# Forward column transform of a Fourier layer over three chunks of rows, each PSUM block with a member (index f) of its own, in place of two chunks with partial sums

## The chip, the cores and the metric

The kernel runs on one core of one Trainium2 chip. A core has five engines that run side by side and meet through semaphores: TensorE (PE in the profile; its weight loads have a row of their own, PEld), VectorE (DVE), ScalarE (ACT), GpSimd (POOL) and SyncE (SP, which here only issues DMAs). TensorE reads its operands from the on-chip memory SBUF and writes its results to the accumulation memory PSUM, from where VectorE or ScalarE has to copy ("evict") them.

The metric is the device time of one execution in microseconds (us). Before the change it is 3847.83 us, the median of three runs (3844.99 to 3849.62). The execution that the profile comes from took 3850.84 us, with a span of 3849.0 us from its first to its last instruction.

## The reference

The input is a batch of 8 images of 8 channels and 256x256 pixels. Two blocks are applied, each with a residual. The first is a grouped Fourier network (4 groups of 10 channels), the second a 3x3 maximum filter:

```python
x = x + fourier_net(group_norm(x))
x = x + dilate3x3(group_norm(x))

def fourier_net(x):                      # 4 groups, 2 channels each, plus two coordinate planes
    h = gconv1x1(concat(x, grid), fc0_w, fc0_b)               # 10 channels per group
    for i in range(4):
        xf = rfft2(h)                                         # only 24 x 12 low modes are used
        lo = einsum('bgixy,gioxy->bgoxy', xf[..., :12, :12], w1[i])
        hi = einsum('bgixy,gioxy->bgoxy', xf[..., -12:, :12], w2[i])
        h = irfft2(place(lo, hi)) + gconv1x1(h, w_w[i], w_b[i])
        if i < 3:
            h = gswish(h)
    h = gswish(gconv1x1(h, fc1_w, fc1_b))                     # 128 hidden channels per group
    return gconv1x1(h, fc2_w, fc2_b)
```

All of it is in float32. Because so few modes are kept, the Fourier transforms are done as products with small tables of cosines and sines.

## The kernel before, in words

**Stages.** Each image goes through four layers. A layer begins with its small spectral part: `spectrum_h` (row transform of what the layer before left in `zt`, L356 and L366), `mix` (the products with the mode weights, L394 and L397) and `rows_of` (inverse row transform into `zt`, L456 or L462, copied by L207). Then comes the loop of `layer` over NCH = 11 chunks of rows, which is where the change is. After the fourth layer the image's state is stored to DRAM, and its head (the 128 hidden channels, fc1 and fc2) is computed later, in 128 steps.

**Two images at once.** The head of image b is not run by itself. `layers` of image b+1 is a generator that yields at marked places, and the driver loop at the end of the kernel answers each `yield (1,)` with one step of the head that is waiting, and each `yield "tail"` with one piece of the dilation of the image before that. So the order on each engine is written out by hand through these yields; the engines take their instructions in exactly this order. The first image has no head beside it (the flag `alone[0]` is true), and after the last image's layers its own head is all that is left.

**A head step** is `first(n)`: four matmuls of 512 columns (L736) into four PSUM banks, evicted by ScalarE in two instructions (L737 one bank, L738 three banks). Every second step, those with odd n, is followed by `second`: eight matmuls (L751) into one bank, which VectorE adds up (L760).

**PSUM.** The eight banks are handed out as two tags with two buffers each: `one` (one bank) and `tri` (three banks). `ps_four` takes one of each. The two buffers of a tag are used in turn, so a user of `tri` waits until the user before the last one has been evicted. A chunk's `burst`, a `first`, a `transform` each take a `one` and a `tri`; `gather` and `second` take a `one` alone.

**The chunk loop.** For each chunk c, `burst(c)` computes the layer's output for that chunk: 16 small matmuls for the 1x1 convolution (L539 in layer 0, L542 in the others) and 8 for the inverse column transform (L545, which reads `zt`), all into one `ps_four`. ScalarE evicts them through the activation into `h` (L550: one instruction of 512 elements per partition, one of 1536). `turn(c)` transposes that chunk in blocks of 32x32 on VectorE (L493, two instructions) into slot c % 3 of `turned`.

The forward column transform then takes two chunks at a time. `transform(k)` runs 32 matmuls of 32 rows by 32 columns (L510). The 256 pixels of a row are split into 8 sections of 32 (index v). Section v goes to the block of 32 PSUM partitions v % 4, so each block gathers only two of the eight sections: four partial sums come out side by side. They are copied to SBUF (L513 on VectorE, L514 on ScalarE), into the third slot of `turned`. `gather(k)` adds the four partial sums with the table `stack` (four identities on top of each other): 4 matmuls over all 128 rows (L524), whose result VectorE copies into `zt` (L527, or L530 twice where the chunks' slots are out of order). With 11 chunks there are five pairs and one single chunk. The same product also brings channel groups and pieces f into the places that the next layer wants: `group_in_f` is true in layers 1 (and 3), false in layers 0 and 2.

Each fp32 matmul is two PE instructions in the trace (a high and a low part), each with its own weight load; counts in the profile are twice those in the code.

Of the kernel before, what the change touches and what calls it, by code (L numbers as in the profile page):

```python
# [21 lines left out]
G = 4  # L22
# [22 lines left out]
def fno_dilate_kernel(ctx: ExitStack, tc: tile.TileContext, a: dict, out: bass.AP):  # L45
# [440 lines left out]
    def layer(b, l, out_, stored, side):  # L486
# [9 lines left out]
        def chunks_of(k):  # L496

            return sorted(range(2 * k, min(2 * k + 2, NCH)), key=lambda c: c % 3)

        def transform(k):  # L500


            cs = chunks_of(k)
            n, lo = len(cs), cs[0] % 3
            step = cs[-1] % 3 - lo if n == 2 else 1
            t = turned[:, lo : lo + step * (n - 1) + 1 : step].rearrange("p n (r v i) -> p n r v i", r=2 * NQ, v=8)
            one, tri, banks = ps_four(f"p_d_{b}_{l}_{k}")
            for v in range(8):
                for q in range(NQ):
                    mm(banks[q][part(v % 4), : 240 * n], fw8[part(q), v, :],  # L510
                       t[part(q), :, :, v, : NBLK * WID], start=v < 4, stop=v >= 4)
            e = turned[:, (2 * k + 1) % 3, : 960 * n].rearrange("p (q x) -> p q x", q=NQ)
            nc.vector.tensor_copy(e[:, 0], one[:, : 240 * n])  # L513
            nc.scalar.activation(e[:, 1:4], tri[:, :, : 240 * n], AF.Identity)  # L514

        def gather(k):

            cs = chunks_of(k)
            n = len(cs)
            e = turned[:, (2 * k + 1) % 3, : 960 * n].rearrange("p (q r f i) -> p q r f i", q=NQ, r=2 * n, f=NQ)  # L520
            p = ps_a(f"p_u_{b}_{l}_{k}")
            for g in range(NQ):
                m = e[:, :, :, g].rearrange("p q r i -> p r q i") if group_in_f else e[:, g]
                mm(p[part(g), : 240 * n], stack, m, start=True, stop=True)  # L524
            src = p[:, : 240 * n].rearrange("p (r g i) -> p r g i", r=2 * n, g=G)
            if cs == sorted(cs):
                nc.vector.tensor_copy(zt[:, 4 * k : 4 * k + 2 * n, :, : NBLK * WID], src)  # L527
            else:
                for i, c in enumerate(cs):
                    nc.vector.tensor_copy(zt[:, 2 * c : 2 * c + 2, :, : NBLK * WID], src[:, 2 * i : 2 * i + 2])  # L530
# [45 lines left out]
        for k in range((NCH + 1) // 2):  # L576
            c = 2 * k
            pair = c + 1 < NCH
# [465 lines left out]
```

## Time and profile before

| | |
|---|---|
| time, median of 3 runs | 3847.83 us (3844.99 to 3849.62) |
| the profiled execution | 3850.84 us, span 3849.0 us |
| PE busy | 3620.7 us (94%), 54200 matmul instructions and as many weight loads |
| DVE busy | 2423.8 us (63%) |
| ACT busy | 2832.3 us (74%) |
| POOL busy | 117.0 us (3%) |
| mean granted PE clock | 0.972 of full speed |
| chain that ended last | PE 76%, DVE 14%, issue 5%, ACT 4%, DMA 1% |
| L510, transform | 9216 instructions, 308.6 us busy |
| L524, gather | 1152 instructions, 136.7 us busy |
| L513 and L514, its evictions | 144 each; ACT 182.9 us |

"Busy" is the time in which at least one instruction of the kind is running; matmuls overlap, so a PE that is shown busy can still be slowed down by what it waits for. "Idle before" a group is the time that the engine stood still just before its instructions, with the engine that ended most of it. The chain that ended last is followed back from the last instruction, at each step to what released it.

By time, a layer's chunk loop takes 53.8 us in all layers 1 and 2 of the images from the second on (first eviction of a burst to the last), and the small spectral part between two loops takes about 63 us. For the first image, which has no head beside it, they take 35.3 us and 43 to 47 us. The last image's layers end at 3551.0 us; the rest is its head.

### The profile page before, as it was taken

Reading aid. Unit: us, or ns where it says so; the run is one execution under the profiler, and the core shown is the slowest. Engines: PE = TensorE matmul, PEld = TensorE weight load, DVE = VectorE, ACT = ScalarE, POOL = GpSimd, SP = SyncE. Lnnn points to the kernel's source line nnn. Section 1 sums busy time; section 2 is a strip of 40 time slices with the busy share of each in tenths; the row PEclk is TensorE's granted clock in tenths of the full one; section 3 lists DMA queues with packets and bytes.
Section 4 is the critical chain, followed back from the end, with each engine's and each line's share of the span. In section 5 each row is a group of like instructions: output and inputs, shape, how many; then the busy total and the mean of one; then the engine's idle time right before and its main releaser. Section 6 shows DMA issues by size and latency. Waiting matters only on the chain.

```text
span 3849.0 us, 119276 instructions
## 1 busy us (share of the span) xinstructions
PE 3620.7 (94%) x54200; PEld 1347.2 (35%) x54200; DVE 2423.8 (63%) x3893; ACT 2832.3 (74%) x2919; POOL 117.0 (3%) x202
## 2 busy tenths in 40 slices
PE   5668999999999999999999999999999999999997
PEld 2333333333333333333333333333333333333222
DVE  6775665556775666766666676665676566673633
ACT  2435777777777777787777777777777777778986
POOL 1000000000000000000000000000000000000100
PEclk7878999999999999999999999999999999999998
DMA  3005111432225222361123612144222532225321
GB/s 88 15 28 193 48 47 45 150 107 61 65 85 178 77 61 61 99 200 55 49 64 110 193 56 58 44 145 154 61 63 59 178 99 63 65 64 182 114 54 51
DMA packets 114089, 345.11 MB, mean 90 GB/s; under 512 B 15984, under 2 KB 18480, under 8 KB 98160
## 3 DMA queue, kind: packets, MB, share of 16 engines
q1 hardware_dynamic: 95392, 276.32, 23.4%
q0 software_dynamic: 18192, 61.17, 5.0%
q8 instruction: 426, 6.98, 0.7%
q14 instruction: 79, 0.65, 0.1%
HBM read 213.43 MB, written 123.74 MB: 88 GB/s over the span
## 4 chain that ended last, share of the span: by engine, by line
PE 76%; DVE 14%; issue 5%; ACT 4%; DMA 1%; POOL 0%; DVEq 0%; POOLq 0%; ACTq 0%
PE p_fc L736 20%; PE p_fc L751 19%; PE p_z L545 10%; PE p_d L510 8%; PE p_z L542 8%; PE p_u L524 3%; PE p_z L539 3%; DVE S L397 3%; DVE turned L394 3%; PE p_b L366 2%; DVE y L760 2%; PE p_g L462 2%; ACT act L738 2%; DVE turned L356 1%; ACT act L737 1%
## 5 line engine op out<-in xcount | busy, mean ns | idle before, releaser
L738 ACT ACTIVATE act<-p_fc 128x1536 f32<-128x1536 f32 x1024 | 1492.6, 1458 | 36.1 <-PE p_fc L736 35.0
L736 PE MATMUL p_fc<-hs,c_w 32*128 32x512 f32 x8192 | 1227.4, 633 | 49.9 <-ACT act L738 13.5
L751 PE MATMUL p_fc<-act,c_w 128*32 128x512 f32 x8192 | 996.1, 602 | 2.0 <-issue 2.0
L737 ACT ACTIVATE act<-p_fc 128x512 f32<-128x512 f32 x1024 | 615.4, 601 | 360.1 <-PE p_fc L736 347.0
L493 DVE STREAM_TRANSPOSE turned<-h 128x1024 f32<-128x1024 f32 x528 | 633.9, 1226 | 250.7 <-ACT h L550 249.9
L550 ACT ACTIVATE h<-p_z 128x512 f32<-128x512 f32 (+1 forms) x528 | 511.9, 1022 | 265.4 <-PE p_z L545 265.4
L736 PEld LDWEIGHTS p_fc<-hs,c_w 32*128 32x128 f32 x8192 | 388.1, 185 | 666.4 <-ACT act L737 230.2
L760 DVE TENSOR_TENSOR y<-p_fc,y 128x512 f32<-128x512 f32 x392 | 267.1, 681 | 551.2 <-PE p_fc L751 551.2
L751 PEld LDWEIGHTS p_fc<-act,c_w 128*32 128x32 f32 x8192 | 215.6, 109 | 713.3 <-issue 376.3
L545 PE MATMUL p_z<-c_binv,zt 32*128 32x256 f32 x5632 | 415.5, 410 | 0.4
L542 PE MATMUL p_z<-h,c_wt 32*32 32x512 f32 x8448 | 367.3, 604 | 6.1 <-ACT act L737 4.2
L545 PEld LDWEIGHTS p_z<-c_binv,zt 32*128 32x128 f32 x5632 | 261.6, 189 | 312.8 <-issue 296.6
L510 PE MATMUL p_d<-turned,c_fw 32*32 32x480 f32 (+1 forms) x9216 | 308.6, 540 | 4.3 <-PE p_z L545 2.9
L514 ACT ACTIVATE turned<-p_d 128x1440 f32<-128x1440 f32 x144 | 182.9, 1270 | 95.2 <-PE p_d L510 92.0
L552 ACT ACTIVATE h<-p_z,c_bias 128x512 f32<-128x512 f32 (+1 forms) x176 | 186.5, 1110 | 76.0 <-PE p_z L545 75.8
L207 DVE COPY zt<-p_g 128x264 f32<-128x264 f32 x304 | 154.7, 604 | 76.6 <-PE p_g L462 46.5
L397 DVE TENSOR_REDUCE S<-turned 128x80 f32<-128x800 f32 x192 | 188.8, 983 | 5.7
L394 DVE TENSOR_TENSOR turned<-t,B 128x800 f32<-128x800 f32 x192 | 188.4, 981 | 0.1
L510 PEld LDWEIGHTS p_d<-turned,c_fw 32*32 32x32 f32 x9216 | 128.2, 103 | 170.2 <-issue 65.1
L356 DVE STREAM_TRANSPOSE turned<-zt 128x960 f32<-128x960 f32 x96 | 177.0, 1870 | 2.9 <-DVE zt L527 0.5
L542 PEld LDWEIGHTS p_z<-h,c_wt 32*32 32x32 f32 x8448 | 92.4, 103 | 188.8 <-ACT act L737 66.6
L524 PE MATMUL p_u<-turned,c_stack 128*32 128x480 f32 (+1 forms) x1152 | 136.7, 543 | 7.2 <-DVE turned L513 6.2
(182 smaller groups left out, 1742.8 us busy)
## 6 DMA issues: line engine op xcount, KB each, us to landing
stored<-h SPq DMA_DIRECT2D x88, 1024.0 KB
hs<-stored SPq DMA_DIRECT2D x352, 256.0 KB
t<-in_spw SPq DMA_DIRECT2D x96, 400.0 KB
yin<-y_rows POOLq DMA_DIRECT2D x56, 512.0 KB, 5.2
h<-in_xp SPq DMA_DIRECT2D x352, 48.0 KB
turned<-in_xw SPq DMA_DIRECT2D x16, 1024.0 KB
y<-in_x SPq DMA_DIRECT2D x56, 256.0 KB
y_rows<-y POOLq DMA_DIRECT2D x56, 256.0 KB, 3.9
```

The source lines that it names most:

```text
L394: nc.vector.tensor_tensor(pr, sw[k], bt[:, k2, k].unsqueeze(2).to_broadcast([128, G, 2 * WID, WID]), ALU.mult)
L397: nc.vector.tensor_reduce(s[k2][:, k].rearrange("p s o g -> p (s o) g"), pr.rearrange("p g m i -> p m g i"), AX.X, ALU.add,)
L493: nc.vector.transpose(dst[:, 2 * i : 2 * i + 2], h[:, c, 2 * i : 2 * i + 2].rearrange("p f (s x) -> p f s x", s=2))
L510: mm(banks[q][part(v % 4), : 240 * n], fw8[part(q), v, :], t[part(q), :, :, v, : NBLK * WID], start=v < 4, stop=v >= 4)
L542: mm(o, wt[part(q), l, g, :], h[part(q), c, f, :], start=True, stop=False)
L545: mm(banks[q][:, HW * s : HW * (s + 1)], zt[part(q), 2 * c + s].rearrange("p f o -> p (f o)"), binv[part(q), :], start=False, stop=s == 1)
L550: nc.scalar.activation(dst, src, AF.Silu)
L736: mm(banks[g], w1[part(g), blk, :], hs[k][part(g), :], start=True, stop=True)
L737: nc.scalar.activation(act[:, 0, :], one, AF.Silu)
L738: nc.scalar.activation(act[:, 1:4, :], tri, AF.Silu)
L751: mm(acc[part(g), :], w2[:, g, 15 - rb - i : 47 - rb - i], act[:, g, :], start=i == 0, stop=i == 1)
L760: nc.vector.tensor_tensor(y, sums, y, ALU.add)
```

## The change

`transform` now takes three chunks at a time (three, three, three and two). A chunk holds four pieces of two pixel rows each (index f). The block of 32 PSUM partitions is now chosen by f, no longer by v % 4, and all eight sections v accumulate in it. So there are no partial sums and `gather` is gone. In place of 32 matmuls with 480 columns for two chunks there are 128 with 180 columns for three.

In layer 1 the result is then already where `zt` wants it, and `put` copies it there (VectorE one bank, ScalarE three). In layers 0 and 2 channel group and piece f have to change places: the result is first copied to SBUF (`swapped`, in slot 2 of `turned`), and the new `swap` sends it once more through TensorE, 16 matmuls of 32x32 with the identities of `stack`, into a further `ps_four`, which `put` then copies to `zt`.

The loop is rewritten to fit. With a head beside it, one chunk is handled per round with one head step each (from the second chunk on); `transform(k - 1)` stands after the step of the first chunk of the next three, ahead of that chunk's `turn`, and `swap(k - 1)` after the step of the second chunk. The number of head steps in a layer's loop and after it is the same, 12; the `"tail"` yields are 11 per layer, before 10. For the first image, `transform(k - 1)` stands after the second chunk's burst, and the first chunk's `turn` is put off until after it.

```diff
--- before.py
+++ after.py
@@ -495,39 +495,51 @@
 
         def chunks_of(k):
 
-            return sorted(range(2 * k, min(2 * k + 2, NCH)), key=lambda c: c % 3)
+            return range(3 * k, min(3 * k + 3, NCH))
+
+        def put(k, one, tri):
+
+            rs = slice(2 * chunks_of(k)[0], 2 * chunks_of(k)[-1] + 2)
+            dst = zt[:, rs, :, : NBLK * WID]
+            n = 60 * len(chunks_of(k))
+            nc.vector.tensor_copy(dst[:, :, 0], one[:, :n].rearrange("p (r i) -> p r i", i=NBLK * WID))
+            nc.scalar.activation(
+                dst[:, :, 1:4].rearrange("p r g i -> p g r i"),
+                tri[:, :, :n].rearrange("p g (r i) -> p g r i", i=NBLK * WID), AF.Identity)
+
+        def swapped(k):
+
+            return turned[:, 2, : 240 * len(chunks_of(k))].rearrange("p (q x) -> p q x", q=NQ)
 
         def transform(k):
 
 
-            cs = chunks_of(k)
-            n, lo = len(cs), cs[0] % 3
-            step = cs[-1] % 3 - lo if n == 2 else 1
-            t = turned[:, lo : lo + step * (n - 1) + 1 : step].rearrange("p n (r v i) -> p n r v i", r=2 * NQ, v=8)
+            n = len(chunks_of(k))
+            t = turned[:, :n].rearrange("p n (s f v i) -> p (n s) f v i", s=2, f=NQ, v=8)
             one, tri, banks = ps_four(f"p_d_{b}_{l}_{k}")
             for v in range(8):
                 for q in range(NQ):
-                    mm(banks[q][part(v % 4), : 240 * n], fw8[part(q), v, :],
-                       t[part(q), :, :, v, : NBLK * WID], start=v < 4, stop=v >= 4)
-            e = turned[:, (2 * k + 1) % 3, : 960 * n].rearrange("p (q x) -> p q x", q=NQ)
-            nc.vector.tensor_copy(e[:, 0], one[:, : 240 * n])
-            nc.scalar.activation(e[:, 1:4], tri[:, :, : 240 * n], AF.Identity)
-
-        def gather(k):
-
-            cs = chunks_of(k)
-            n = len(cs)
-            e = turned[:, (2 * k + 1) % 3, : 960 * n].rearrange("p (q r f i) -> p q r f i", q=NQ, r=2 * n, f=NQ)
-            p = ps_a(f"p_u_{b}_{l}_{k}")
-            for g in range(NQ):
-                m = e[:, :, :, g].rearrange("p q r i -> p r q i") if group_in_f else e[:, g]
-                mm(p[part(g), : 240 * n], stack, m, start=True, stop=True)
-            src = p[:, : 240 * n].rearrange("p (r g i) -> p r g i", r=2 * n, g=G)
-            if cs == sorted(cs):
-                nc.vector.tensor_copy(zt[:, 4 * k : 4 * k + 2 * n, :, : NBLK * WID], src)
+                    for f in range(NQ):
+                        mm(banks[q][part(f), : 60 * n], fw8[part(q), v, :],
+                           t[part(q), :, f, v, : NBLK * WID], start=v == 0, stop=v == 7)
+            if group_in_f:
+                put(k, one, tri)
             else:
-                for i, c in enumerate(cs):
-                    nc.vector.tensor_copy(zt[:, 2 * c : 2 * c + 2, :, : NBLK * WID], src[:, 2 * i : 2 * i + 2])
+                e = swapped(k)
+                nc.vector.tensor_copy(e[:, 0], one[:, : 60 * n])
+                nc.scalar.activation(e[:, 1:4], tri[:, :, : 60 * n], AF.Identity)
+
+        def swap(k):
+
+            if group_in_f:
+                return
+            e = swapped(k)
+            one, tri, banks = ps_four(f"p_u_{b}_{l}_{k}")
+            for j in range(NQ):
+                for g in range(NQ):
+                    mm(banks[g][part(j), : 60 * len(chunks_of(k))], stack[part(g), :], e[part(g), j],
+                       start=True, stop=True)
+            put(k, one, tri)
 
         def burst(c):
             one, tri, banks = ps_four(f"p_z_{b}_{l}_{c}")
@@ -573,44 +585,40 @@
                 if c > 3 and not alone[0]:
                     read_x(b + 1, c - 4)
             return
-        for k in range((NCH + 1) // 2):
-            c = 2 * k
-            pair = c + 1 < NCH
+        for c in range(NCH):
+            k, i = divmod(c, 3)
             burst(c)
-            if k > 1:
-                gather(k - 2)
             if alone[0]:
+                if k > 0 and i == 1:
+                    transform(k - 1)
+                    turn(c - 1)
+                if k > 0 and i == 2:
+                    swap(k - 1)
+                if k == 0 or i:
+                    turn(c)
+                if c == NCH - 1:
+                    swap(k - 1)
+                continue
+            if c == 0:
+                yield "tail"
                 turn(c)
-                if pair:
-                    burst(c + 1)
-                if k > 0:
-                    transform(k - 1)
-                if pair:
-                    turn(c + 1)
                 continue
-            if k == 1:
-                transform(0)
-            if k > 0:
+            if k > 0 and i == 0:
                 yield (1,)
+                transform(k - 1)
+                turn(c)
             else:
-                yield "tail"
-            turn(c)
-            if k > 1:
-                transform(k - 1)
-            if k > 0:
-                for _ in range(2 if pair else 1):
-                    yield "tail"
-            if pair:
-                burst(c + 1)
-                turn(c + 1, (0,))
-            yield (1,)
-            if pair:
-                turn(c + 1, (1,))
+                turn(c, (0,))
+                yield (1,)
+                turn(c, (1,))
+            yield "tail"
+            if k > 0 and i == 1:
+                swap(k - 1)
         out_["sw"] = [load_sw(l + 1, k) for k in range(3)]
-        gather(k - 1)
-        transform(k)
         yield (1,)
-        gather(k)
+        transform(3)
+        yield (1,)
+        swap(3)
 
     def start(b, out_):
         if b < n_img:
```

## The prediction

> **What bounds the kernel now.** First the page: shares, clock and chain.
>
> ```profile
> span 3849.0 us, 119276 instructions
> ...
> PE 3620.7 (94%) x54200; PEld 1347.2 (35%) x54200; DVE 2423.8 (63%) x3893; ACT 2832.3 (74%) x2919; POOL 117.0 (3%) x202
> ...
> PE 76%; DVE 14%; issue 5%; ACT 4%; DMA 1%; POOL 0%; DVEq 0%; POOLq 0%; ACTq 0%
> ```
>
> TensorE is the bound, but the change sits in the chunk loop, so I asked for the busy times of one such loop (image 4, layer 1) and of the stretch after it.
>
> ```profile
> 1873.70:1927.50 53.80, 53.60 (x929) 20.46 (x925) 40.08 (x49) 43.60 (x44) 3.13 (x5) 1.00 0.17 51
> 1927.50:1990.10 62.60, 60.56 (x734) 21.16 (x733) 39.28 (x63) 46.00 (x48) 0.54 (x1) 1.00 0.23 67
> ```
>
> After the stretch come its length and the busy us of PE, PEld, DVE, ACT and POOL, then the clock. In the loop PE has no gap, full clock; DVE and ACT have 10 us to spare. Next the timeline of two chunks in that loop (start, length; PE and ACT rows).
>
> ```profile
> 1892.66 1.14 PE L736 MATMUL p_fc<-hs,c_w 32*128 32x512 f32 x8
> ...
> 1893.73 2.19 PE L510 MATMUL p_d<-turned,c_fw 32*32 32x480 f32 x58
> ...
> 1894.32 1.45 ACT L738 ACTIVATE act<-p_fc 128x1536 f32<-128x1536 f32 x1
> ...
> 1895.37 0.59 PE L542 MATMUL p_z<-h,c_wt 32*32 32x512 f32 x1
> ...
> 1895.80 1.28 PE L542 MATMUL p_z<-h,c_wt 32*32 32x512 f32 x31
> ...
> 1897.98 1.04 PE L736 MATMUL p_fc<-hs,c_w 32*128 32x512 f32 x8
> ...
> 1898.17 1.94 ACT L550 ACTIVATE h<-p_z 128x512 f32<-128x512 f32 x2 [0.74 <-PE p_z L545]
> ...
> 1898.95 1.92 PE L751 MATMUL p_fc<-act,c_w 128*32 128x512 f32 x16
> ```
>
> Start to start, a burst costs PE 2.17 us (L542 1.10, L545 1.07), a first 1.07, a second 1.85 (1898.95 to 1900.80), a gather 0.95. ACT needs 1.94 us for a burst and 1.95 for a first. The two L542 lines matter most: the burst issued one matmul and then stood until 1895.80, just after ACT's L738 ended at 1895.77. That is the `tri` rule: a unit waits for the eviction of the unit before the last. Before the change this costs little, because each pair of chunks is gather, first, transform, burst, first, second, burst: between a unit and the next but one there is always about 2 us of other PE work.
>
> Last, how fast 32x32 matmuls stream (timeline rows of four whole groups).
>
> ```profile
> 2316.21 1.49 PE L462 MATMUL p_g<-c_rowg,fz 32*32 32x66 f32 x128
> ...
> 2188.45 0.88 PE L419 MATMUL p_f<-fs,c_fold 32*32 32x72 f32 x64
> ...
> 1933.49 1.44 PE L510 MATMUL p_d<-turned,c_fw 32*32 32x240 f32 x64
> ...
> 1927.47 2.29 PE L510 MATMUL p_d<-turned,c_fw 32*32 32x480 f32 x64
> ```
>
> Record by record, in the first and the last two of these 17 matmuls go out (34 weight loads), then PE pauses; the 18th goes out 0.33, 0.62 and 1.02 us after the first. That is 0.22 us plus two passes of N/1.2 ns (0.11, 0.40, 0.80). Inside a window a matmul follows after 16.6 ns. The low pass starts N/1.2 + 25 ns after the high one. Check on 64 matmuls of N=66: 3 windows (0.99) + 12 x 0.0166 + 0.08 + 0.22 (the last one's length) = 1.49 us, the row shown.
>
> **What the Trainium skill says.** "TensorE: Matmul & The Clock Gate", The mechanism (Part 3), gives PE a 64-deep window; 17 matmuls of four instructions are 68, so the trace agrees. The same page's Measured speedup vs the span model has 16 tiles cost one matmul's length plus 4 ns for each further tile; the trace has 7 to 17 ns and the pause, which that does not hold. "TensorEngine Tiling (Array Packing)", PSUM Bottleneck, warns that faster TensorE leaves the PSUM copy as the limit; the wait at 1895.37 shows it here.
>
> **The change, part by part, per layer with a head beside it.**
>
> Transform. N=180: a window is 0.22 + 0.30 = 0.52 us. 128 matmuls are 7 windows and 8 more: 3.64 + 0.13 to the last start, and with its low pass 3.95; the next unit can enter from 3.8 on, so I take 3.9. The last one, N=120: 7 x 0.42 + 0.13 + 0.125 + 0.10 = 3.3, and 0.1 to change the tile shape (1933.49 to the next L736 at 1934.87 is 1.38, where the same sum gives 1.28): 3.4. Together 3 x 3.9 + 3.4 = 15.1 us. Before: five of about 2.08 (2.06 before a burst, 2.21 before a first) and one of 1.38: 11.8. So +3.3. Equal columns, in smaller pieces: the pause between windows comes 28 times, not 6.
>
> Gather. Removed: five of 0.95 and one of 0.80: -5.55.
>
> Swap (layers 0, 2): 16 matmuls of N=180, less than one window: 0.11 issue + 0.175 + 0.15 + 0.1 = about 0.5 us, four times: +2.0.
>
> PE work: layer 1 -2.25 us, layers 0 and 2 -0.25 us.
>
> Waits. I laid the new order out unit by unit, with ACT in order and a unit starting only when the unit before the last is evicted. The steps at chunks 1, 3, 5, 7, 9 carry a second (32 steps per layer, so the parity holds), those at 2, 4, 6, 8, 10 don't. Burst, first, next unit without a second: the first covers 1.07 of the burst's 0.09 + 1.94 eviction, so PE stands 1.0 us. In layer 1 that happens five times (before bursts 3, 5, 9, before transform 1 and before step 11): +5.0. With a swap it is worse: the swap waits 1.0 us for the burst's eviction, and the burst after it needs the first's eviction, which ACT ends 4.0 us after the burst, when PE is ready at 2.5: another 1.45. At chunks 4 and 10: 4.9 us; at chunk 7, which has a second, 0.55; before burst 3, transform 1 and burst 9: 3.0. Sum 8.4.
>
> Net: layer 1 -2.25 + 5.0 = +2.7, layers 0 and 2 -0.25 + 8.4 = +8.1. Seven images: 7 x 2.7 + 14 x 8.1 = +132 us.
>
> First image, alone. Bursts cover each other here (2.17 against 1.94). But chunk 3k's turn now queues behind transform(k-1): DVE then has three turns (7.1 us) before the next transform, and at the end turns 9 and 10 (4.8 us) stand between transform 2 and 3. My layout gives 48 us against about 46 per layer: +2 to 3, three times, +8 (0 to 15).
>
> Evictions. Per layer ACT loses 7.6 us of L514 and gets, from 1.37 us at 1440 and 0.77 at 720 elements (0.17 + 0.83 ns each), 0.62 us per three chunks, twice with a swap: 2.3 or 4.7. DVE loses 7.6 us and gets 1.3 or 2.6. Both are worth nothing: PE covers them (40.1 and 43.6 of 53.8 us). The turn behind the transform delays DVE by up to 3.9 us; queued behind it are adds, which PE needs two `one` buffers later, over 2 us off. The last swap delays the transposes of L356; the stretch after the loop is filled by PE (60.56 of 62.6), so I cost it at nothing; uncovered, 1 us per layer, 21 us. Transform 3 needs turn 10, which DVE ends some 4.5 us after burst 10; PE has 5 us of other work and waits before it. On SP's queue the three weight loads stay between loop and last transform; POOL's DMAs come with the tails, one of which moves forward per layer.
>
> Sum: +132 + 8 = +140. Also, a wait of 0.4 us per layer of the old order falls away (the burst after transform 0, whose L542 row takes 1.61 us at 1884.23 instead of 1.16), -8, so about +132 on the profiled 3850.8. Its median is 3 us lower: **3980 us**.
>
> **Rivals.**
>
> *No waits (faster).* If eviction kept ahead, only PE work counts: 7 x -2.25 + 14 x -0.25 + 8 = -11 us; and with the next rival's transform -108, so 3740 to 3837. It decides if the waits come to under about 0.5 us a layer. Against it: ACT's triple eviction alone is 1.45 us, a first 1.07, and at 1895.37 PE does wait. Only if a unit's `tri` came free sooner could it hold.
>
> *The window does not bind.* Tiles then bound it: 16 passes of 0.1525 plus start, 2.7 us, and 2.4 for the last: 3 x 1.2 + 1.0 = 4.6 us less per layer, 21 layers, -97: 3885. For: only groups of 32 matmuls exist at large N, the four-window case has N=66. Against: three sizes on one line.
>
> *More than counted.* PE's instruction stream quadruples in a transform (512 in 3.9 us); if fetching lags, or DVE's adds come late, 2 to 5 us per layer: 4020 to 4090.
>
> *No difference*: gains and waits cancel; needs the second rival and half of the waits.
>
> **How the numbers follow.** Window and waits as counted 58% (3940 to 4030); window not binding 15% (3860 to 3940); more 12%; no waits 12%; cancelling 3%. Likeliest: 3980. The range drops the fast cases and the far end of "more": 3885 to 4045. Faster by over 0.2% 0.12, within 0.2% (what a measurement of this kernel can tell from no change) 0.03, slower 0.85.
>
> **What would show it.** L523 with 24576 instructions, about 4.25 us from a transform's start to its last end, 17 matmuls at a time. No L524. In layer 1's loop bursts split into one matmul and, 1 us later, the rest, with ACT as releaser; in layers 0 and 2 L540's groups start late too; chunk loops, 53.8 us before, of about 58 us in layer 1 (three transforms of 3.9 for four of 2.07 and three gathers of 0.95: +0.6; four waits: +4) and 61 in layer 2 (two swaps 1.0, their waits 2.0). ACT's and DVE's busy times lower by some 90 and 130 us. Wrong if a transform takes under 3 us, or if bursts after a lone first start at once.

## The result, and the profile after

The changed kernel takes 4273.07 us (median of 4 runs, 4263.00 to 4282.79) against 3848.72 us (median of 4, 3844.99 to 3854.38): a ratio of 1.1101, with a 95% interval of 1.1071 to 1.1130. It is slower, as forecast, but by 424 us and not by 132, and lies far outside the range of 3885 to 4045 us. Of all executions behind this document one, of run 8 below, fell into a slow state (10348.86 us) and is left out of that run's ratio.

The page of the changed kernel, the lines that were shown of the kernel before (from here on L523 is the transform, L540 the swap, L551 in layer 0 and L554 in the others the first matmuls of a burst, L562 the burst's eviction by ScalarE, L505 the copy of `put` on VectorE, L744 a head step's `first`, L759 its `second`; an edit shifts some of them by a few lines):

```profile
span 4269.7 us, 151682 instructions
...
PE 3871.2 (91%) x70456; PEld 1600.5 (37%) x70456; DVE 2293.7 (54%) x3717; ACT 2734.0 (64%) x2935; POOL 117.1 (3%) x202
...
PE 68%; DVE 13%; ACT 9%; issue 8%; DMA 2%; POOL 0%; DVEq 0%; POOLq 0%; ACTq 0%
```

DVE lost 130 us and ACT 98, as forecast (130 and 90). But PE is busy 251 us longer, and idle on top of that; in the chain, ScalarE went from 4% to 9% and "issue" (an engine that waits for nothing which the profile shows) from 5% to 8%.

The same windows as before, for image 4: the chunk loop of layer 0, the loop of layer 1 and the stretch after it, and the loop of layer 2, each with its length, the busy us of PE, PEld, DVE, ACT and POOL, and the granted PE clock (the number that follows POOL's):

```profile
1941.00:2018.00 77.00, 70.53 (x1481) 32.09 (x1478) 37.55 (x59) 40.81 (x46) 1.83 (x3) 0.84 0.14 43
...
2087.50:2151.10 63.60, 58.74 (x1410) 27.79 (x1408) 34.58 (x41) 39.70 (x44) 3.13 (x5) 1.00 0.20 64
2151.10:2213.60 62.50, 59.08 (x843) 22.45 (x848) 39.57 (x62) 44.17 (x47) 0.54 (x1) 1.00 0.17 48
2213.60:2281.30 67.70, 60.43 (x1476) 28.43 (x1474) 35.20 (x43) 40.90 (x46) 3.13 (x5) 0.97 0.20 60
```

Layer 1's loop takes 63.6 us where 53.8 had been and 58 were forecast; PE, which had no gap there, now stands still for 4.9 us of it. Its stretch is as long as before. Layer 0's loop takes 77.0 us at a clock of 0.84; the same loop in the kernel before:

```profile
1749.90:1810.50 60.60, 59.95 (x933) 22.45 (x933) 41.11 (x63) 43.60 (x44) 1.83 (x3) 0.92 0.11 32
```

Over images 2 to 8, from a layer's first burst eviction to the next layer's: layer 0 took 849.3 us before and 1026.2 after (+177.0), layer 1 815.9 and 877.7 (+61.8), layer 2 829.0 and 967.3 (+138.2). The first image grew by 34.9 us and the fourth layers' loops by 7.6. That is nearly the whole difference: 419 of the 421 us between the two spans.

Now the timeline, TensorE alone, of a lone head step and of a transform in layer 1 of image 5:

```profile
2608.84 1.04 PE L744 MATMUL p_fc<-hs,c_w 32*128 32x512 f32 x8
2609.81 1.04 PE L554 MATMUL p_z<-h,c_wt 32*32 32x512 f32 x2
2611.03 1.15 PE L554 MATMUL p_z<-h,c_wt 32*32 32x512 f32 x30 [0.18 <-ACT h L562]
...
2614.04 1.92 PE L759 MATMUL p_fc<-act,c_w 128*32 128x512 f32 x16
2615.89 3.25 PE L523 MATMUL p_d<-turned,c_fw 32*32 32x180 f32 x193
2620.06 1.07 PE L523 MATMUL p_d<-turned,c_fw 32*32 32x180 f32 x53 [0.91 <-issue]
```

The first three lines are the wait that the prediction describes: after a head step without a second, the burst issues one fp32 matmul (two instructions) and stands until ScalarE's eviction ends. The last two it had only as a rival. The transform runs for 193 instructions at the rate foreseen and stops for 0.91 us, with every operand there and no semaphore to wait for. TensorE's list of waits, in the whole run (us in total, times, longest), has it on top:

```profile
PE p_d L523 <- issue: 83.9, 83, 2.0
...
PE p_fc L744 <- DVE zt L505: 17.6, 12, 1.6
...
PE p_u L540 <- ACT h L562: 15.5, 24, 0.7
PE p_d L523 <- ACT h L562: 14.9, 21, 0.7
```

I call these stops holes. From the start of one matmul to the start of the next, the 96 transforms hold 76 of more than 0.7 us at full clock, median 1.25 us, 101 us in sum; the transforms of the kernel before hold none. The seven of three chunks that ran at full clock without a hole take 3953 ns in the median (3952 to 4484) from their first start to their last.

What arrives around them can be read off the trace's instruction queue. It moves blocks of 16384 bytes, 426 in the kernel before and 553 after; TensorE's matmuls and weight loads over 256 make 423 and 550, and with the few other records of its two rows 426.4 and 553.4. So one block is 256 of TensorE's instructions. The Trainium skill, "Runtime: NRT & Kernel Launch", Instruction fetch mechanics, gives the same size, and says of the crossing into a new block that its cost is mostly hidden. In this trace it isn't: two fetches never start less than 3.29 us apart (95% of them 3.45 us or more), while a transform hands out 512 instructions in 3.95 us, and a hole ends, in the median, 2.38 us after a fetch has started (2.19 to 2.90). The hole above ends at 2620.06; the fetch before it started at 2617.63. The place of the holes ties them to the blocks: counted through all records of TensorE's two rows from the first one on, in groups of 256, the matmul that ends a hole has 193 (53 times) or 194 (23 times) records of its group before it, in all 76 holes. In the fifteen kernels of this document taken together 1143 of TensorE's 1158 "issue" stops after the first burst stand at 193 to 195; the other 15 are one stop before L366 in each kernel's first image.

The second thing the page's digits hardly show is the clock. Summed over the trace's records, TensorE was granted half its clock for 215.9 us before and for 482.1 us after. Of the 266 us more, images 2 to 8 have 110.4 in layer 0's loops (37.5 to 147.9), 97.9 in the stretches after layers 0 and 2 (6.8 to 104.7), and the first image about 39. Half the clock for a time T costs at most T/2, where TensorE's speed is the limit: at most 133 us. Each figure of half clock comes from one profiled execution; in a stage that an edit leaves alone it moves by up to 10 us (the stretches after layer 1: 3.4 us here, 13.7 in run 3).

### The profile page after: what moved, and what is told of

Read it like the earlier page. It is cut to its first block, busy times and chain, and to the rows that moved or that the text cites. A ratio compares the mean times of both kernels' runs of the same rounds, so it can differ in the third digit from the quotient of the medians.

```text
span 4269.7 us, 151682 instructions
## 1 busy us (share of the span) xinstructions
PE 3871.2 (91%) x70456; PEld 1600.5 (37%) x70456; DVE 2293.7 (54%) x3717; ACT 2734.0 (64%) x2935; POOL 117.1 (3%) x202
## 4 chain that ended last, share of the span: by engine, by line
PE 68%; DVE 13%; ACT 9%; issue 8%; DMA 2%; POOL 0%; DVEq 0%; POOLq 0%; ACTq 0%
PE p_fc L759 18%; PE p_fc L744 17%; PE p_d L523 10%; PE p_z L557 9%; PE p_z L554 7%; ACT h L562 5%; PE p_z L551 3%; ACT act L746 2%; DVE S L397 2%; PE p_b L366 2%; DVE turned L394 2%; DVE turned L493 2%; DVE y L768 2%; PE p_g L462 1%; DMA yin<-y_rows 1%
## 5 line engine op out<-in xcount | busy, mean ns | idle before, releaser
L746 ACT ACTIVATE act<-p_fc 128x1536 f32<-128x1536 f32 x1024 | 1493.4, 1458 | 53.8 <-PE p_fc L744 52.8
L744 PE MATMUL p_fc<-hs,c_w 32*128 32x512 f32 x8192 | 1292.4, 644 | 75.3 <-DVE zt L505 17.6
L759 PE MATMUL p_fc<-act,c_w 128*32 128x512 f32 x8192 | 1026.3, 618 | 6.5 <-DVE zt L505 5.4
L562 ACT ACTIVATE h<-p_z 128x512 f32<-128x512 f32 (+1 forms) x528 | 512.1, 1021 | 373.6 <-PE p_z L557 373.6
L744 PEld LDWEIGHTS p_fc<-hs,c_w 32*128 32x128 f32 x8192 | 421.4, 189 | 637.2 <-ACT act L745 228.5
L523 PE MATMUL p_d<-turned,c_fw 32*32 32x180 f32 (+1 forms) x24576 | 438.8, 317 | 108.6 <-issue 83.9
L759 PEld LDWEIGHTS p_fc<-act,c_w 128*32 128x32 f32 x8192 | 219.9, 112 | 751.4 <-issue 416.5
L557 PE MATMUL p_z<-c_binv,zt 32*128 32x256 f32 x5632 | 437.8, 425 | 1.2 <-issue 0.7
L554 PE MATMUL p_z<-h,c_wt 32*32 32x512 f32 x8448 | 407.6, 610 | 26.6 <-issue 8.9
L523 PEld LDWEIGHTS p_d<-turned,c_fw 32*32 32x32 f32 x24576 | 330.3, 105 | 264.4 <-issue 138.2
L557 PEld LDWEIGHTS p_z<-c_binv,zt 32*128 32x128 f32 x5632 | 273.0, 196 | 335.6 <-issue 318.4
L530 ACT ACTIVATE turned<-p_d 128x540 f32<-128x540 f32 x64 | 37.4, 584 | 323.7 <-PE p_d L523 142.0
L529 DVE COPY turned<-p_d 128x180 f32<-128x180 f32 x64 | 21.1, 330 | 303.5 <-PE p_d L523 303.5
L554 PEld LDWEIGHTS p_z<-h,c_wt 32*32 32x32 f32 x8448 | 96.1, 103 | 215.6 <-ACT h L562 63.6
```

The costliest lines, as they stand in the source:

```text
L523: mm(banks[q][part(f), : 60 * n], fw8[part(q), v, :], t[part(q), :, f, v, : NBLK * WID], start=v == 0, stop=v == 7)
L554: mm(o, wt[part(q), l, g, :], h[part(q), c, f, :], start=True, stop=False)
L557: mm(banks[q][:, HW * s : HW * (s + 1)], zt[part(q), 2 * c + s].rearrange("p f o -> p (f o)"), binv[part(q), :], start=False, stop=s == 1)
L562: nc.scalar.activation(dst, src, AF.Silu)
L744: mm(banks[g], w1[part(g), blk, :], hs[k][part(g), :], start=True, stop=True)
L746: nc.scalar.activation(act[:, 1:4, :], tri, AF.Silu)
```

## The experiments

Each is timed beside the kernel before on the same chip; that one moved little from one set of runs to the next (3848.30 to 3852.11 us). "Half clock" is as above.

**1 to 4. The holes, the rows, the swap.** In the kernel before, each transform matmul cut into four (128 of 120 columns, as many instructions as in the changed kernel):

```diff
-            for v in range(8):
-                for q in range(NQ):
-                    mm(banks[q][part(v % 4), : 240 * n], fw8[part(q), v, :],
-                       t[part(q), :, :, v, : NBLK * WID], start=v < 4, stop=v >= 4)
+            for r in range(4):
+                for v in range(8):
+                    for q in range(NQ):
+                        o = banks[q][part(v % 4), : 240 * n].rearrange("p (n r i) -> p n r i", n=n, r=2 * NQ)
+                        mm(o[:, :, 2 * r : 2 * r + 2], fw8[part(q), v, :],
+                           t[part(q), :, 2 * r : 2 * r + 2, v, : NBLK * WID], start=v < 4, stop=v >= 4)
```

> The kernel before, with one edit: each transform's 32 matmuls of 480 columns are cut into 128 of 120 (the single chunk's into 128 of 60). Order, gathers, evictions, buffers are untouched. Window law alone: 7 windows of 0.42 us plus 0.4 make 3.3 us in place of 2.06, +1.2 us for each of six transforms a layer, 24 layers: about +170 us. Supply theory (PE's instructions come in blocks of 256, at best one per 3.4 us, as the DMA records after the change show, and 512 in 3.3 us run dry once): a hole of 1 to 1.7 us in most transforms, +170 more, so about +340 us. If the holes come from something else in the new loop (its buffers, its order), they are absent here and the time is near +170.

4496.25 us, ratio 1.1684 (1.1650 to 1.1718): +646. Cutting alone, in the old order, with the gather kept and no swap, brings the holes. From the lists of groups of the kernel before and of this one:

```profile
L510 PE MATMUL p_d<-turned,c_fw 32*32 32x480 f32 (+1 forms) x9216 | 308.6, 540 | 4.3 <-PE p_z L545 2.9 <-DVE turned L493 1.1
```

```profile
L512 PE MATMUL p_d<-turned,c_fw 32*32 32x120 f32 (+1 forms) x36864 | 535.6, 267 | 284.6 <-issue 284.2
```

Busy time rises by 227 us (more windows of 17 matmuls, for which 170 were expected), idle time by 280, all of it "issue". The holes have a median of 1.88 us here, where the window law has the 512 instructions used up in 3.3 us and not in 3.95; all 130 at full clock end at 193 or 194 of a group of 256. Half clock rose by 239 us, at most 119 us of time; with the two that makes 626 of the 646 us, where I had expected 340. The 626 count a little twice, as 33 us of the half clock lie within the transforms' busy time.

The opposite edit, in the changed kernel, leaves out sections 4 to 7 of every transform, half of its matmuls:

```diff
-            for v in range(8):
+            for v in range(4):
...
-                           t[part(q), :, f, v, : NBLK * WID], start=v == 0, stop=v == 7)
+                           t[part(q), :, f, v, : NBLK * WID], start=v == 0, stop=v == 3)
```

> The changed kernel with the transforms cut to sections 0 to 3 of the eight, so 64 matmuls each in place of 128 (sections 4 to 7 are left out of the sum). Window law: 3 windows and 0.4 us = 1.95 us in place of 3.95, -2.0 us for each of 96 transforms = -190 us. Supply theory: 256 instructions in 2 us need only one block more, so the holes (1.0 to 1.5 us in most transforms, about 100 us in all) go as well, and with them most of the half clock: -330 us or more. If the holes have nothing to do with the number of instructions, they stay, and the time falls by 190 us.

3921.88 us, ratio 1.0192 (1.0162 to 1.0221): -351 against the changed kernel. The transform's group:

```profile
L523 PE MATMUL p_d<-turned,c_fw 32*32 32x180 f32 (+1 forms) x12288 | 226.5, 320 | 25.5 <-ACT h L562 15.0 <-DVE turned L493 9.9 <-issue 0.6
```

"Issue" went from 83.9 to 0.6 us, while the waits on ScalarE stayed (14.9 and 15.0). A transform takes 1943 ns (the median of 47 without a stop), half of 3953. The work left out is worth some 185 us by the prediction's durations (24 layers of 7.7); the other 166 are the holes (about 96 us, below), at most 42 us of half clock (482.1 to 398.1) and some 28 us that I can't assign.

Third, the rows: in layer 0's first matmuls of a burst (L551), all 32 rows of each block of 32 partitions instead of 6, from the second image on (the weights of the added rows are zero):

```diff
-                        k = slice(32 * q, 32 * q + 6)
+                        k = slice(32 * q, 32 * q + 6) if b == 0 else part(q)
```

> The changed kernel; layer 0's 1x1 matmuls use all 32 rows of their tile from the second image on in place of 6 (the added weights are zero, so the result is the same; as many instructions, as many columns). If layer 0's loops are slow (77 us against 67 in layer 2) because few active rows and the holes together let the clock drop to half, the 148 us of half clock in those seven loops fall to the 10 us of layer 2's, and the time by 40 to 70 us. If the clock follows gaps in time alone, nothing changes (within 10 us).

4227.03 us, ratio 1.0985 (1.0950 to 1.1019): -46. The loop of layer 0, image 4, to set beside the one of 77.00 us:

```profile
1933.70:2003.40 69.70, 61.24 (x1478) 29.05 (x1478) 37.50 (x59) 40.79 (x46) 1.83 (x3) 1.00 0.15 47
```

The clock is 1.00, with the same holes and waits; over all images layer 0's loops went from 147.9 to 6.8 us of half clock. The stretches after layers 0 and 2 kept most of theirs (85.3 of 104.7).

Fourth, the swap left out in layers 0 and 2; the transform's outputs go straight to `zt`, unswapped:

```diff
-            if group_in_f:
+            if True:
                 put(k, one, tri)
@@ in swap @@
-            if group_in_f:
-                return
+            return
```

> The changed kernel with the swap left out in layers 0 and 2: the transform's result is copied straight to its place as in layer 1 (so group and piece stay unswapped there). As in the prediction's sum: swaps 2.0 us and their waits 3.4 us per layer, 16 layers: -85 us. If the copies that queue on VectorE behind a turn and a tail, and the half clock in the stretch after layers 0 and 2 (53 and 51 us of it) belong to the swap as well, the stretches after the loops fall to layer 1's 62 us and the time by 150 us or more.

4092.05 us, ratio 1.0634 (1.0603 to 1.0665): -181 where the prediction's terms give 85. The stretches after layers 0 and 2 fall from 491.1 and 497.0 to 448.5 and 449.9 us, within 6 us of the kernel before, and the waits on L505 are gone. Half clock falls by 170 us, to 312.4, half of it in layer 0's loops. The 85 of the terms, the waits of 23.0 us on L505 and at most 85 us of clock are enough for what was measured; how much of it the clock is was not measured.

What the swap does to VectorE is seen in layer 0 of image 5 of the changed kernel:

```profile
2510.97 0.60 PE L540 MATMUL p_u<-turned,c_stack 32*32 32x180 f32 x32
...
2512.78 1.23 DVE L493 STREAM_TRANSPOSE turned<-h 128x1024 f32<-128x1024 f32 x1
...
2515.13 0.69 DVE L831 TENSOR_TENSOR o<-o,yin 128x512 f32<-128x512 f32 x1
2515.74 0.34 DVE L505 COPY zt<-p_u 128x180 f32<-128x180 f32 x1
...
2516.13 1.78 PE L744 MATMUL p_fc<-hs,c_w 32*128 32x512 f32 x8 [1.62 <-DVE zt L505]
```

The swap's matmuls end at 2511.57, but the copy out of its single bank (L505) stands in VectorE's queue behind a turn and a piece of the dilation and starts at 2515.74. The head step wants that bank and waits for 1.62 us.

**5. The same instructions in halves.** In the changed kernel each transform of a layer with a head beside it is cut in two, sections 0 to 3 and 4 to 7, with the lone head step between; swaps and some turns move with it:

```diff
...
+            if c in (4, 6, 10):
+                m = {4: 0, 6: 1, 10: 2}[c]
+                transform(m, (0,))
+                yield (1,)
+                transform(m, (1,))
...
-        transform(3)
+        transform(3, (0,))
         yield (1,)
+        transform(3, (1,))
         swap(3)
```

> The changed kernel with each transform of layers 0 to 2 cut in two halves (column blocks 0 to 3, then 4 to 7), with the lone head step between them; the same instructions on TensorE, in another order, the swaps a chunk later. Theory that TensorE outruns the supply of its instructions in the 3.95 us of 512 instructions: a half has 256 of them and a head step lies between, so, as in the run with half the matmuls, the holes of 1.2 us go (83 of them, -80 to -105 us), and with the head step's work queued between, ScalarE's evictions are waited for less and the half clock shrinks too: -130 to -250 us against the changed kernel, 4025 to 4145 us. Theory that the holes come from something that a transform's matmuls need (its operands, its banks, the number of matmuls in flight): the holes stay in number (more than 40 of 83), and the time moves by less than 60 us: above 4210 us.

4124.49 us, ratio 1.0721 (1.0705 to 1.0736): -149 against the changed kernel. TensorE's waits before the transform's matmuls:

```profile
PE p_d L526 <- DVE y L786: 38.1, 14, 3.3
PE p_d L526 <- DVE turned L494: 24.5, 31, 3.6
...
PE p_d L526 <- issue: 17.0, 34, 1.1
```

"Issue" falls from 83.9 to 17.0 us with not one instruction less. Of the 17.0 us, 7.3 are in the first image, where no head step lies between the halves; in the other images 9.7 us are left of 78.4. So the holes are no price of the matmuls themselves; they come with 512 instructions in a row at this rate, and seldom with 256. What is new are waits on VectorE, 62.6 us, which my moved turns brought.

**6 and 7. An even spread of the second matmuls, a test that failed.** Four matmuls behind every head step in place of eight behind every other one, in the changed kernel and, as a control, in the one before:

```diff
...
-            if n % 2 and n > 2:
-                second(n - 3)
+            if n > 1:
+                second(n - 2)
```

> The changed kernel with the head's second matmuls spread evenly: four behind every head step, with an addition of their own, instead of eight behind every other one. Theory of the waits (a lone head step between two bursts is too short for ScalarE's two evictions): each loop of layer 1 gains up to its 5.0 us and each of layers 0 and 2 about 3.9 of 8.4, about -90 us, 4160 to 4210 us, the holes in the transforms unchanged in number and length (about 70, sum 105 us). Rival, that ScalarE's evictions are not what costs time in the loops, but holes and clock only: within 25 us of the changed kernel, 4250 to 4300 us. The 512 more additions of 0.7 us on VectorE are off the path in both, unless the copies out of the swaps queue behind them: then slower than 4300 us.

> The kernel before with the same even spread of the second matmuls, the control for the run above: its loops show next to no waits on ScalarE's evictions, so the spread has nothing to take away: within 15 us of 3849 us in both theories. If it gains more than 30 us here, the gain above is not that of the waits which the change brought.

4386.62 us (ratio 1.1396, 1.1378 to 1.1415) and 4071.44 us (1.0576, 1.0561 to 1.0590): both far slower, the control by 223 us where 0 was expected. The edit brings its own wait, in the kernel before as well: a second now takes a `one` bank in every round, so that a burst needs the bank of the head step just before it, whose eviction has not come yet. In the control's list of groups the idle time before L736 (`first`) rose from 49.9 to 113.6 us (53.4 of it on L737, the eviction of its single bank), and 103 bursts wait for L737 ahead of their first matmul, 64.4 us in all, where the kernel before has 4.2. VectorE's additions, now twice as many, are waited for too: TensorE stands 35.1 us for them before the second matmuls. So the edit tells nothing of the waits in question. Runs 12 and 13 take its place.

**8. Full rows in the kernel before.**

> The kernel before with all 32 rows of each stripe in layer 0's first matmuls for the second image on (the added rows of the weights are zero). In the changed kernel the same edit took the half clock in layer 0's loops from 147.9 to 6.8 us, at -46 us in all. The kernel before has 37.5 us of half clock there. Theory that matmuls of 6 rows are what lowers the clock: these 37.5 us go, and with them up to half of that in time: -5 to -19 us, 3830 to 3845 us. Rival, that in the kernel before the half clock of this stage has another cause: the half clock stays above 25 us and the time within 4 us of 3849 us.

3835.64 us against 3848.30, ratio 0.9960 (0.9947 to 0.9973). Layer 0's loop of image 4, 60.6 us before, is at full clock:

```profile
1749.90:1805.90 56.00, 55.12 (x937) 21.24 (x933) 40.88 (x63) 43.64 (x44) 1.84 (x3) 1.00 0.11 35
```

The 37.5 us of half clock in these loops are gone. This version is faster than both kernels, by 0.4% against the one before.

**9 and 10. Several at once.** The split and the full rows, and then without the swap too:

> The split transforms and, from the second image on, all 32 rows of each stripe in layer 0's first matmuls (the added rows of the weights are zero), both in the changed kernel. The split left 99.0 us of half clock in layer 0's loops, which the rows alone took from 147.9 to 6.8. If holes and the low-row clock are separate causes, the rows take this 99.0 to under 15 and 30 to 46 us more: 4070 to 4100 us. If the two share one cause, less than 15 us more than the split's 4124: 4110 to 4130 us.

> As the run before it, and without the swap: in layers 0 and 2 the transform's outputs go straight to the place that the swap's would take (the exchange of blocks is left out). It closes the account: holes, low-row clock and swap all taken away. By layer 1, where the split leaves +7.0 us a layer over the kernel before, the three layers then each cost about that: 21 times 7, less some 17 us of the half clock that the kernel before has in layer 0, plus some 20 to 30 us of the first image: 3960 to 4020 us, with half clock near the 216 us of the kernel before (under 260). If a further cause sits in layers 0 and 2, above 4030 us.

4096.39 us (ratio 1.0632, 1.0616 to 1.0648) and 4019.82 us (1.0428, 1.0401 to 1.0455). The rows give 28 us on top of the split by the medians and 34 by the ratios, within or just short of the 30 to 46 expected, and take layer 0's half clock from 99.0 to 3.4, so the holes and the clock of the six-row matmuls are separate causes. Without the swap the time is at the edge of what was expected (3960 to 4020) and the half clock, 281.7 us, above it (under 260); 171 us of span are left over the kernel before: 5.7, 7.9 and 6.3 us for layers 0, 1 and 2 of each of seven images, 139 in all, and about 31 us in the first image. In the list of waits, 57.8 us stand for transforms that wait for a turn, 9.3 in the changed kernel; the split put these turns off.

**11. The swap's first quarter by ScalarE.**

```diff
...
+            if by_act:
+                nc.scalar.activation(dst[:, :, 0], one[:, :n].rearrange("p (r i) -> p r i", i=NBLK * WID), AF.Identity)
+            else:
...
-            put(k, one, tri)
+            put(k, one, tri, by_act=True)
```

> The changed kernel with the swap's first quarter copied out by ScalarE instead of VectorE, so that nothing of the swap waits in VectorE's queue behind turns and normalization. The waits of TensorE on that copy (17.6 and 5.4 us) go. If these idle stretches are what lowers the clock in the stages after layers 0 and 2 (104.7 us of half clock), that falls under 50 us: -30 to -65 us in all, 4210 to 4245 us. If the clock there has another cause, the half clock stays above 70 us and the gain is that of the waits alone, or is given back to ScalarE, which has 0.35 us more for each swap: 4245 to 4285 us.

4230.59 us, ratio 1.0981 (1.0944 to 1.1017): -42. The waits on L505 (23.0 us) are gone, and the two stretches are 22.8 us shorter. Half clock in them fell from 104.7 to 75.5 us, above the bound of 70: by the clock, these waits are not its main cause there. The time lies where it was expected if they were (4210 to 4245 us), so it alone does not decide, and the fall of 29 us is not far above the scatter of such figures.

**12 and 13. A shorter eviction.** To take away what TensorE waits for, without touching TensorE: in layers 0 to 2 of images 2 to 8 ScalarE's second eviction of a burst covers one bank of three (the activation of the other two is left out, older values stay in their places), in the changed kernel and in the one before:

```diff
-            for dst, src in ((h[:, c, 0, :], one), (h[:, c, 1:4, :], tri)):
+            w = 1 if b > 0 and l < 3 else 3
+            for dst, src in ((h[:, c, 0, :], one), (h[:, c, 1 : 1 + w, :], tri[:, :w])):
```

> The changed kernel with ScalarE's second eviction of each burst cut to one of its three banks in layers 0 to 2 of images 2 to 8 (the activation of the other two is left out, their places keep older values): a burst's eviction is then about 1.2 us instead of 1.94, nothing on TensorE is changed. Theory of the waits: layer 1's five waits go (-3.7 us a layer), layers 0 and 2 lose some 4.5 of their 8.4, since a swap's burst still waits for the head step's eviction: about -90 us, between -60 and -130 with what the clock gains; the holes in the transforms stay (about 80, 100 us). Rival, that the order's waits cost little and the loss lies in holes and clock alone: less than 30 us gained, above 4240 us.

> The kernel before with the same cut of a burst's eviction (the activation of two of its four banks left out in layers 0 to 2 of images 2 to 8), as the control: its loops leave TensorE no gap, so a shorter eviction has next to nothing to take away: within 15 us of the kernel before. If it gains more than 40 us, the gain in the run above is not that of waits which the change brought.

4160.80 us (ratio 1.0820, 1.0800 to 1.0841), -112 against the changed kernel, and 3839.21 us (0.9974, 0.9966 to 0.9982), -10. A chunk of layer 1, image 4, to set beside the one shown after the change:

```profile
2053.95 1.04 PE L745 MATMUL p_fc<-hs,c_w 32*128 32x512 f32 x8
2054.92 1.51 PE L554 MATMUL p_z<-h,c_wt 32*32 32x512 f32 x32
```

The burst after the lone head step runs as one group. Layer 1's loops lose 3.9 us each (3.7 expected); the control's lose 1.4, of which 0.8 come back in the stretch behind, so that the waits' own share is about 3 us. Of the 20 bursts of layer 1 that stood for over 0.7 us after their first matmul none is left. The holes stay:

```profile
PE p_d L523 <- issue: 87.6, 87, 1.9
```

So waits and holes are two causes: here the waits go without the holes, and in run 2 the holes without the waits.

## Why the prediction was wrong

**The transform's duration** was right and wrong. The law of windows, drawn from other sizes, gave 3.95 us, and 3953 ns were measured where no hole fell in, 1943 against 1.95 for half a transform. "The window does not bind" falls. That the window's 68 instructions are the 64-deep one was a loose fit, which no run here tests. But the next sentence, "so I take 3.9", took this law for the only limit. **This is the step that failed first.** The rival "more than counted" named the cause ("PE's instruction stream quadruples in a transform"), put it at 2 to 5 us per layer together with late additions, and gave it 12%. The waits list's "issue" on L523 and on the bursts behind it (83.9, 8.9 and 3.4 us) makes about 96 us: 4 us per layer, in 24 layers. A count of instructions per us, 130 in the new transform (512 in 3.95) against 34 in the loop before (929 matmuls and 925 loads in 53.8 us), could be made from what was shown. Where the limit lies it does not say, but the kernel before had run into it: its list of waits has

```profile
PE p_g L462 <- issue: 8.7, 7, 1.8
```

L462 is the line of 32x32 matmuls from whose rows the law of windows was partly drawn. All seven of these stops stand at 193 or 194 of a group of 256 and end 2.26 to 2.62 us after a fetch has started, as the holes do.

**The waits** were right in place and nearly in size: before the bursts, the transform and the swap that it listed. The shorter eviction gained 102 us more than its control, where the edit was expected to remove about 90 of the 153 us counted; up to 24 us of that may be clock.

In layer 1, where half clock hardly disturbs (3.4 us in seven images), the sum nearly closes: 2.7 us forecast per layer (its waits as forecast, not as measured), 4.2 us of holes in its transforms (24 of them over seven images, 32.9 us, less the 0.15 us that each pause has anyway) and 0.5 of "issue" before the bursts behind them make 7.4; 8.8 were measured.

**The clock** is the second step that failed, by silence: every duration was taken at full clock, since the windows shown had 1.00. Layer 0's loop was not among them; its window, at 0.92, would have shown that the clock is not always full. The rows alone are worth 46 us in the changed kernel.

**The swap** was costed as 16 matmuls and waits for ScalarE, 85 us, and measured at 181. "I cost it at nothing" for the stretch after the loop was wrong in layers 0 and 2: these stretches grew by 6.9 and 6.4 us per layer, 93 us in all, where 21 were given for the case that the cover is gone. The copy that the swap queues on VectorE behind a turn and a tail was missed: the prediction listed what the turn delays, but not what the swap's own copy has in front of it. It costs 23 us of waits. Of the other 73 us of the swap's excess over its terms the record shows only that 170 us of half clock, at most 85 us of time, went away with the swap.

**The first image** was +8 (up to 15) and came to 35: by its share of the holes, and up to 20 us of clock (39 us more at half).

With about 96 us of holes, 96 of the swap beyond its terms, 46 of the rows' clock and 27 of the first image, the forecast's 132 make 397 of 421 us. The parts overlap in the clock and in the first image's holes, so this is an account and no proof; some 24 us are not assigned.

**Open.** What lowers the clock was not settled. Three different edits (rows, swap, split) each take a part of the half clock away, and with all of them 281.7 us are left, 66 more than before. But 51 of these 66 are in the first image, which the rows and the split do not touch; images 2 to 8 are at 65 us, where they had 48 before and 273 after the change. The Trainium skill, "TensorE: Matmul & The Clock Gate", A second HAM failure mode, tells of a kernel (there in bf16) whose TensorE idles briefly and often between groups of matmuls and swings between half and full clock; this agrees with what is seen here. TensorE stands still for 47.6 us in layer 0's loops of images 2 to 8 where it had 4.8, and no stop is longer than 1.62 us. But layer 2's loops stand still longer (52.3 us) at 10.2 us of half clock only, so in layer 0 it takes the six-row matmuls besides. Why a fetch comes too late, and whether fewer or shorter instructions could make a block last longer, was not tried.

## What to carry to other kernels

Before cutting a TensorE stage into more and smaller matmuls, count its instructions, weight loads included, against time: here a run of 512 in 4 us stopped for 1.25 us in most cases, while the same instructions in runs of 256, with a head step's eight large matmul instructions between, seldom did. A stop of TensorE for "issue" in the profile of the kernel before can be a sign of this limit, however small its sum; count whether several of them stand at the same place in a group of 256 instructions. When one unit is moved or inserted, follow its copy-out through the evicting engine's queue, and ask for each pair of units with shared PSUM buffers whether the work between covers the eviction. Look at the granted clock of every stage that a change touches, not of a sample.

## What the hardware showed that I had not expected

- TensorE's instructions arrive in blocks of 256, at least 3.29 us apart in the changed kernel; faster use ends there in stops of up to 2.0 us, always at the same place of a block (193 or 194 of 256 in all 76 holes), and in 284 us of stops in the kernel with 128 matmuls of 120 columns per transform.
- Matmuls with 6 active rows of 32 go with half the clock where small stops come in between: 147.9 us of it in layer 0's loops, 6.8 with zero rows added, at no cost in TensorE's time; in the kernel before, which has hardly any stops, 37.5 and 0.
- The clock falls to half (147.9 us of it in layer 0's loops, 104.7 in the stretches after layers 0 and 2) though TensorE never stands still for more than 1.62 us in the ones and 1.81 in the others; half clock comes in pieces of 3.4 us and multiples of it.
